# FP4 network between two attentions: where its inputs are quantized, and where the next attention's operands begin

## Chip, core and metric

The kernel runs on one core of a Trainium2 chip. The metric is the device time of one execution in microseconds. PE is the matmul engine (PEld its weight loads), DVE the vector engine, ACT the engine of activation functions, POOL the general-purpose engine, SP the engine from whose queue most DMAs are issued.

## The reference, cut to what matters

Eight batches of 512 tokens with 128 features go through four blocks; after each, the block's input is added and the sum is normalized.

```python
x = _layernorm(x + _L0_attn_ref(x, ...))   # 16 heads of 8, score bias by distance
x = _layernorm(x + _L0_ffn_ref(x, ...))    # FP4 network
x = _layernorm(x + _L1_attn_ref(x, ...))   # 16 heads of 8, no score bias
x = _layernorm(x + _L1_ffn_ref(x, ...))    # two layers of local attention and GEGLU

def fp4_quant_dequant(x):                  # blocks of 16 along the last dim
    scale = max(max(abs(xb)) / 6, 1e-12)
    xn = xb / scale
    return GRID[searchsorted(MID, abs(xn))] * sign(xn) * scale   # 0 .5 1 1.5 2 3 4 6
def _L0_ffn_ref(x, w_gate, w_up, w_down):  # 128 -> 352 -> 128
    q = fp4_quant_dequant
    h = silu(q(x) @ q(w_gate).T) * (q(x) @ q(w_up).T)
    return q(h) @ q(w_down).T
```

## The kernel before, in words

The activations stay on chip: `xn` and `xs` hold all eight batches, `xn` the normalized values and `xs` the sums before normalizing. The four blocks follow one another: `attention(0)`, `ffn0`, `attention(1)`, `ffn1`. A block opens its own pools of tiles on chip and closes them at its end, so the tiles of one block lie where those of the block before lay.

**Order.** Each engine has a queue. The program's scheduler chooses the order in a queue. An instruction wrapped in `keep_in_program_order` stays behind everything written before it for its engine; the attention's matmuls and transposes (`mm`, `tr`, lines 126 and 127) are wrapped so, as are the late loads on SP (`held`, line 78). The rest is free.

**An attention** (lines 121 to 352). For a batch, `begin_x` transposes `xn` to `xT`; `begin_qk` projects q and k, splits each into two parts on POOL (lines 167 and 168) and writes them to DRAM (`far`); `load_qk` reads them back into `qs_` and `ks_` in another layout; `begin_v` projects v into `va`, whose rest is zeros and a column of ones. Then a list of steps runs: eight per unit, four units per batch, 256 for eight batches, and 36 more in which the last units end. In step `s` the scores of one block of queries are made twice: PE makes `s_ps` and DVE takes its row maximum (line 239); 16 steps later PE makes the transposed scores `t_ps` and ACT takes the exponential into a tile `e` (line 245). `todo` holds what else a step does: the row of maxima is sent into `qs_` by a DMA from POOL's queue (line 257), the values are summed, the sums divided, projected, added and normalized (`end_o`, `end_y`). The next batch's operands begin ten steps ahead. The first batch's are made before the first step. Four PSUM banks of `p_t` are shared by `t_ps` and all the smaller products.

**The FP4 network** (lines 355 to 454). It loads the weights, quantizes them and transposes them into `wgu` and `wd`. `quantized` (line 361) does a blockwise quantization: DVE takes the maximum of each block (371) and makes scales and their inverses (372, 373, 375), POOL multiplies by the inverse (376), DVE isolates the exponent by an integer operation (377), makes from it a number to add and take away again (378, 379, 380), which rounds, and POOL multiplies by the scale (381). For each batch `begin` quantizes `xn`; `gated` transposes the result and makes the gate and up products, their product `h` and its quantization in two halves; `down` transposes it, multiplies by `wd`, adds and normalizes (by ACT, line 112). The next batch's `begin` and the down product of the batch before follow each `gated`.

Of the kernel before, what the change touches and what calls it, by code (L numbers as in the profile page):

```python
# [18 lines left out]
P = 128  # L19
B, S, D = 8, 512, 128  # L20
NT = S // P
G = 4
# [18 lines left out]
def body(ctx, tc, x, consts, rows, wa0, wa1, acols, bo, wf, wqkv, wo, w1, w2, cols, b2r, qs, ks, out):  # L41
# [77 lines left out]


    def attention(li, alibi, qs_, ks_, late=None):
# [6 lines left out]
        with ExitStack() as st:  # L128
# [11 lines left out]
            qb = const.tile([P, 1], F32, name="qb")  # L140
            nc.vector.tensor_tensor(qb, col[:, 0:1], col[:, 1:2], ALU.mult)
            va = []
            for i in range(2):
                v = const.tile([P, NT, 16, 32], F32, name=f"va{i}")
                nc.gpsimd.memset(v, 0.0)
                nc.gpsimd.memset(v[:, :, :, 8:9], 1.0)
                va.append(v)


            def begin_x(b, h):  # L150
                ps = bank("xt_ps")
                for c in range(NT):
                    tr(ps[:, c * P : (c + 1) * P], xn[:, b * NT + c, :], ident)
                h["xT"] = work.tile([P, S], F32, tag="xT", name="xT", bufs=1)
                nc.vector.tensor_copy(h["xT"], ps)

            def begin_qk(b, h, n):
                ps = bank("qk_ps")
                mm(ps, lhsT=w[:, n * P : (n + 1) * P], rhs=h["xT"], start=True, stop=True)
                t = work.tile([P, S], F32, tag=f"x{n}", name="x", bufs=1)  # L160
                if n == 0:
                    nc.scalar.activation(t, ps, AF.Identity, bias=qb, scale=col[:, 0:1])  # L162
                else:
                    nc.scalar.activation(t, ps, AF.Identity, bias=col[:, 2:3])
                parts = work.tile([P, 2, S], F32R, tag=f"hl{n}", name="parts", bufs=1)
                hi, lo = parts[:, 0, :], parts[:, 1, :]
                nc.gpsimd.tensor_copy(hi, t)  # L167
                nc.gpsimd.tensor_tensor(lo, t, hi.bitcast(F32), ALU.subtract)

                far = dram.tile([2, 2, 64, S], F32R, tag=f"far{n}", name="far")  # L170
                for j in range(2):
                    nc.sync.dma_start(
                        out=far[j].bitcast(F32).rearrange("a c t -> c a t"), in_=parts[64 * j : 64 * j + 64].bitcast(F32)
                    )
                h["far", n] = far

            def load_qk(b, h, n, part):

                dst, pp = (qs_, ks_)[n][b % 2], slice(4 * part, 4 * part + 4)
                for j in range(2):  # L180
                    both = h["far", n][j].bitcast(F32).rearrange("a (p d) t -> a d p t", d=8)
                    for r in range(4):
                        at = 64 * j + 8 * r
                        nc.sync.dma_start(
                            out=dst[at : at + 8, pp].bitcast(F32), in_=both[r // 2 if n == 0 else r % 2][:, pp]
                        )

            def begin_v(b, h):
                h["o"] = work.tile([P, NT, P], F32, tag="o", name="o", bufs=3)
                ps = bank("v_ps").rearrange("p (c d) -> p c d", c=NT)  # L190
                for c in range(NT):
                    mm(ps[:, c, :], lhsT=h["xT"][:, c * P : (c + 1) * P], rhs=w[:, W_V : W_V + P], start=True, stop=True)
                nc.scalar.copy(va[b % 2][:, :, :, 0:8], ps.rearrange("p c (h d) -> p c h d", d=8))
# [115 lines left out]
            batch, units = [{} for _ in range(B)], []  # L309
            for n in range(B * G):  # L310
# [7 lines left out]
                if g == 0 and b + 1 < B:  # L318

                    early = max(s - 10, 1)  # L320
                    later(early, begin_x, b + 1, batch[b + 1])
                    later(early + 2, begin_qk, b + 1, batch[b + 1], 0)
                    later(early + 4, begin_qk, b + 1, batch[b + 1], 1)
                    for part in range(2):
                        for j in range(2):
                            later(s + 6 + 12 * part + 2 * j, load_qk, b + 1, batch[b + 1], j, part)
                    later(s + 20, begin_v, b + 1, batch[b + 1])
                    later(s + 20, with_bias, b + 1)
                if g == G - 1:
                    later(z + 15, end_o, batch[b])  # L330
                    later(z + 18, end_y, b, batch[b])

            begin_x(0, batch[0])
            begin_qk(0, batch[0], 0)
            begin_qk(0, batch[0], 1)
            for part in range(2):
                for j in range(2):
                    load_qk(0, batch[0], j, part)
            begin_v(0, batch[0])
# [3 lines left out]
            with_bias(0)  # L343
            if late:
                late()
            for s in range(B * G * NU + LAG + 20):
# [3 lines left out]
                for f, a in todo.pop(s, []):  # L350
                    f(*a)
            assert not todo


    def ffn0():
        with ExitStack() as st:
            pool = lambda name, bufs, **k: st.enter_context(tc.tile_pool(name=f"f{name}", bufs=bufs, **k))
            const, work = pool("c", 1), pool("w", 2)
            p_g, p_t = pool("g", 2, space=PSUM), pool("t", 4, space=PSUM)

            def quantized(src, n, tag):

                nb = n // 16
                blocks = lambda t: t.rearrange("p (n k) -> p n k", k=16)
                over = lambda t: t.unsqueeze(2).broadcast_to([P, nb, 16])
                tile_ = lambda name, w: work.tile([P, w], F32, tag=f"{name}{tag}", name=name)
                sc, inv, y, m = tile_("sc", nb), tile_("inv", nb), tile_("y", n), tile_("m", n)  # L370
                nc.vector.tensor_reduce(sc, blocks(src), AX.X, ALU.max, apply_absolute_value=True)
                nc.vector.tensor_scalar(sc, sc, float(np.float32(1.0) / np.float32(6.0)), 1e-12, ALU.mult, ALU.max)
                nc.vector.reciprocal(inv, sc)

                nc.vector.tensor_scalar_mul(inv, inv, 1.0 - 2.0**-23)
                nc.gpsimd.tensor_tensor(blocks(y), blocks(src), over(inv), ALU.mult)
                nc.vector.tensor_single_scalar(m.bitcast(I32), y.bitcast(I32), 0x7F800000, ALU.bitwise_and)
                nc.vector.tensor_scalar(m, m, 1.0, 1.5 * 2.0**22, ALU.max, ALU.mult)
                nc.vector.tensor_tensor(y, y, m, ALU.add)
                nc.vector.tensor_tensor(y, y, m, ALU.subtract)  # L380
                nc.gpsimd.tensor_tensor(blocks(y), blocks(y), over(sc), ALU.mult)
                return y


            wgu = const.tile([P, 2, NI], F32, name="wgu")
            wd = const.tile([P, 3, D], F32, name="wd")
            wraw = const.tile([P, F_ALL], F32, name="wraw")
            nc.sync.dma_start(out=wraw, in_=wf)
            for j in range(2):
                wq = quantized(wraw[:, j * 3 * P : (j + 1) * 3 * P], 3 * P, "w")  # L390
                ps = p_t.tile([P, 3 * P], F32, tag="tr", name="w_ps")
                for c in range(3):
                    nc.tensor.transpose(ps[:, c * P : (c + 1) * P], wq[:, c * P : (c + 1) * P], ident)
                nc.scalar.copy(wgu[:, j, :], ps[:, 0:NI])
            wq = quantized(wraw[:, 6 * P : F_ALL], NI, "w")
            ps = p_t.tile([P, 3, P], F32, tag="tr", name="wd_ps")
            for c, (at, n) in enumerate(I_CH):
                nc.tensor.transpose(ps[0:n, c, :], wq[:, at : at + n], ident)
            for c, (at, n) in enumerate(I_CH):
                nc.scalar.copy(wd[0:n, c, :], ps[0:n, c, :])  # L400

            def begin(b):
                return quantized(xn[:, b * NT : (b + 1) * NT, :].rearrange("p c d -> p (c d)"), S, "x")

            def gated(b, xq):
# [6 lines left out]
                for half in range(2):  # L412
# [12 lines left out]
                    hq.append(quantized(h.rearrange("p t i -> p (t i)"), 2 * NI, "h"))  # L425
# [19 lines left out]
            xq = begin(0)  # L445
            before = None
            for b in range(B):
                hq = gated(b, xq)
                if b + 1 < B:
                    xq = begin(b + 1)  # L450
                if before:
                    down(*before)
                before = (b, hq)
            down(*before)
# [334 lines left out]
    with tc.tile_pool(name="ops", bufs=1) as ops:  # L789
# [14 lines left out]
        def first_late():  # L804
            constant_rows(1, held)
            load_late()

        constant_rows(0, nc.sync.dma_start)
        attention(0, True, qs_, ks_, first_late)
# [3 lines left out]
        ffn0()  # L813
        attention(1, False, qs_, ks_)
# [98 lines left out]
```

## Time and profile before

| | |
|---|---|
| Time of three runs, median (lowest to highest) | 2124.07 us (2123.54 to 2126.24) |
| The profiled execution's own time, its span | 2124.89 us, 2123.1 us |
| Mean granted TensorE clock | 0.914 of full speed |
| Busy, share of the span: PE, DVE, ACT, POOL | 82%, 71%, 54%, 39% |
| First attention, first to last step | about 36 to 562 us |
| FP4 network, with its weights | about 573 to 762 us |
| Second attention | about 762 to 1240 us |
| Last block | about 1240 to 2123 us |

Durations below come from the profiled execution. A row of a group names line, engine, operation, output and inputs by the program's names, the shapes and the count; then the busy time and the mean of one; then the idle time of its engine just before it and what ended that. A row of the timeline gives start and duration; an arrow in brackets names what the engine waited for. Instructions on one engine can overlap a little, so durations sum to more than busy time.

### The profile page before, as it was taken

What the parts mean: (1) busy time and instruction counts of PE and PEld (TensorE: products, weight loads), DVE (VectorE), ACT (ScalarE), POOL (GpSimd) and SP (SyncE); (2) the same over time, 40 slices, a digit from 0 to 9 for tenths busy, and PEclk for the clock granted to TensorE, in tenths of its full rate; (3) what the DMA queues carried; (4) which work ended last, traced back from release to release, by engine and by line L of the source; (5) the groups of instructions that cost most, each with busy time, mean ns of one, the idle gap of its engine ahead of it and who ended that gap; (6) DMA issues with size and microseconds to landing.
All of it is one profiled execution on the core that took longest, in us unless ns stands there. A gap on an engine that the chain in (4) does not pass through costs nothing.

```text
span 2123.1 us, 38263 instructions
## 1 busy us (share of the span) xinstructions
PE 1742.1 (82%) x14229; PEld 970.8 (46%) x14245; DVE 1501.2 (71%) x3156; ACT 1151.4 (54%) x2717; POOL 829.1 (39%) x880
## 2 busy tenths in 40 slices
PE   1899999999666549999999966888889889898894
PEld 0444444444244424333333333555655566565562
DVE  2577777777488737888888726777777777788752
ACT  0266666666422215777777723556656656656560
POOL 3312222212444451222221134465555555666653
PEclk6599999999877758999999967999999999999997
DMA  6532232220000024232221001111111111111110
GB/s 116 164 61 51 52 61 53 44 48 2 12 1 1 0 61 97 59 58 60 58 59 36 2 25 25 28 31 28 29 34 28 29 29 33 34 40 34 31 31 20
DMA packets 91628, 88.45 MB, mean 42 GB/s; under 512 B 45825, under 2 KB 57473, under 8 KB 91442
## 3 DMA queue, kind: packets, MB, share of 16 engines
q1 hardware_dynamic: 86752, 85.00, 18.2%
q8 instruction: 113, 1.85, 0.4%
q0 software_dynamic: 4096, 0.54, 0.2%
q14 instruction: 73, 0.60, 0.1%
q10 hardware_dynamic: 594, 0.47, 0.1%
HBM read 41.33 MB, written 18.87 MB: 28 GB/s over the span
## 4 chain that ended last, share of the span: by engine, by line
PE 23%; DVE 22%; ACT 13%; POOL 2%; issue 2%; DMA 1%; SPq 0%; ACTq 0%; POOLq 0%; DVEq 0%
ACT pw L463 8%; PE s_ps L126 7%; PE av L126 6%; DVE t L564 4%; DVE r L560 4%; DVE ss L568 3%; DVE m L624 3%; DVE m L239 3%; PE qk_ps L461 2%; ACT sq L463 2%; PE t_ps L126 2%; DVE nrm L587 1%; DVE u L739 1%; PE qk_ps L126 1%; PE p_ps L462 1%
## 5 line engine op out<-in xcount | busy, mean ns | idle before, releaser
L239 DVE TENSOR_REDUCE m<-s_ps 128x1 f32<-128x512 f32 x1024 | 647.8, 685 | 226.4 <-PE s_ps L126 117.6
L245 ACT ACTIVATE e<-t_ps 128x512 f32<-128x512 f32 x1024 | 552.8, 595 | 241.1 <-PE t_ps L126 235.8
L126 PE MATMUL s_ps<-k,q 63*128 63x512 f32 x1024 | 384.9, 511 | 106.9 <-DVE m L239 65.6
L126 PEld LDWEIGHTS s_ps<-k,q 63*128 63x128 f32 x1024 | 151.5, 192 | 399.7 <-DVE m L239 288.5
L463 ACT ACTIVATE pw<-sp,m,nrm 128x128 f32<-128x128 f32 x512 | 226.3, 462 | 180.2 <-DVE m L626 174.7
L126 PE MATMUL t_ps<-q,k 64*128 64x512 f32 x1024 | 286.4, 426 | 0.4 <-ACT e L245 0.2
L126 PE MATMUL av<-e,va 128*32 128x512 f32 x2048 | 275.2, 608 | 0.0
L257 POOL DMA_DIRECT2D q<-mt x128 | 68.4, 538 | 505.8 <-ACT mt L253 505.8
L637 POOL TENSOR_TENSOR pw<-pw,den 128x1024 f32<-128x1024 f32 x64 | 121.2, 1894 | 211.5 <-DVE den L636 164.6
L571 POOL TENSOR_TENSOR r<-r,t 128x1024 f32<-128x1024 f32 x64 | 150.9, 2358 | 98.8 <-DVE t L564 96.5
L560 DVE TENSOR_TENSOR r<-qk_ps,tab 128x512 f32<-128x512 f32 x128 | 87.4, 682 | 102.0 <-ACT sq L463 102.0
L461 PE MATMUL qk_ps<-wqkv_s,hT 128*128 128x512 f32 x256 | 140.2, 676 | 16.3 <-DVE t L564 15.5
L126 PEld LDWEIGHTS t_ps<-q,k 64*128 64x128 f32 x1024 | 127.1, 188 | 16.7 <-ACT e L245 16.5
L462 PE MATMUL p_ps<-cst,pw 128*128 128x128 f32 x512 | 76.4, 284 | 51.2 <-DVE xs L702 28.5
L463 ACT ACTIVATION_READ_ACCUMULATOR pw<-sp,m,nrm 128x1 f32 x512 | 106.9, 209 | 0.0
L464 ACT COPY v<-v_ps 128x512 f32<-128x512 f32 x64 | 37.5, 586 | 108.4 <-PE v_ps L461 108.4
L564 DVE TENSOR_TENSOR t<-qk_ps,tab 128x256 f32<-128x256 f32 x256 | 95.4, 414 | 0.0
L668 DVE COPY pT<-p_ps 128x512 f32<-128x512 f32 x128 | 84.3, 686 | 15.3 <-PE p_ps L462 14.7
L126 PEld LDWEIGHTS <-sel 64*128 64x128 bf16 x2048 | 69.3, 97 | 52.1 <-issue 39.3
L126 PE MATMUL s_ps<-tri,sel 64*128 64x64 bf16 x1024 | 91.7, 199 | 0.0
L167 POOL CAST parts<-x 128x512 fp32r<-128x512 f32 x32 | 19.4, 607 | 182.2 <-ACT x L162 176.8
L463 ACT ACTIVATE sq<-qk_ps 128x1024 f32<-128x1024 f32 x64 | 68.4, 1069 | 34.7 <-PE qk_ps L461 34.6
(161 smaller groups left out, 3229.1 us busy)
## 6 DMA issues: line engine op xcount, KB each, us to landing
far<-parts SPq DMA_DIRECT2D x64, 256.0 KB
q<-far SPq DMA_DIRECT2D x256, 64.0 KB
k<-far SPq DMA_DIRECT2D x256, 64.0 KB
ve<-v SPq DMA_DIRECT2D x112, 128.0 KB
xn<-in_x SPq DMA_DIRECT2D x8, 256.0 KB
q<-mt POOLq DMA_DIRECT2D x128, 4.0 KB, 2.8
hn<-xs SPq DMA_DIRECT2D x16, 128.0 KB
out<-xn SPq DMA_DIRECT2D x8, 256.0 KB
```

Source lines behind the costliest of these rows:

```text
L126: mm = lambda *a, **k: tc.keep_in_program_order(nc.tensor.matmul(*a, **k))
L239: nc.vector.tensor_reduce(u["m"][:, j, pp, blk : blk + 1], ps[j], AX.X, ALU.max)
L245: nc.scalar.activation(e, ts[j], AF.Exp, scale=float(SLOPES[2 * vp + j]) if alibi else 1.0)
L257: nc.gpsimd.dma_start(out=q[at : at + 1, 2 * g : 2 * g + 2, :].bitcast(F32).rearrange("o a (c t) -> o (a c) t", t=P), in_=mt[8 * j : 8 * j ...
L461: mm = lambda *a, **k: tc.keep_in_program_order(nc.tensor.matmul(*a, **k))
L462: tr = lambda *a, **k: tc.keep_in_program_order(nc.tensor.transpose(*a, **k))
L463: act = lambda *a, **k: tc.keep_in_program_order(nc.scalar.activation(*a, **k))
L560: nc.vector.tensor_tensor(heads(r[:, n]), heads(ps[:, n]), cos.unsqueeze(1).broadcast_to([P, HEADS, DH]), ALU.mult)
L564: nc.vector.tensor_tensor(heads(t2[:, n])[:, :, a : a + 32], heads(ps[:, n])[:, :, 32 - a : 64 - a], sin[:, a : a + 32].unsqueeze(1).broad ...
L571: nc.gpsimd.tensor_tensor(r, r, t2, ALU.add)
L637: nc.gpsimd.tensor_tensor(pw.rearrange("p s r k -> p (s r) k"), pw.rearrange("p s r k -> p (s r) k"), den.rearrange("p s r -> p (s r)").un ...
L668: nc.vector.tensor_copy(h["pT"][:, s], ps)
```

## The change

`quantized` moves out of the network, gets its buffers from its caller, and writes its result where the caller says. The integer operation is replaced by an absolute value on ACT, and the two constants after it change:

```diff
-                nc.vector.tensor_single_scalar(m.bitcast(I32), y.bitcast(I32), 0x7F800000, ALU.bitwise_and)
-                nc.vector.tensor_scalar(m, m, 1.0, 1.5 * 2.0**22, ALU.max, ALU.mult)
+        nc.scalar.activation(m, y, AF.Abs)
+        nc.vector.tensor_scalar(m, m, 1.5, 2.0**22, ALU.max, ALU.mult)
```

The weights are quantized in the first attention, before its first step, in nine of the 13 `e` tiles; their transposes use banks of `p_t` and are not wrapped. The network's own copies of this are gone.

```diff
+    def tokens(b):
+        return xs[:, b * NT : (b + 1) * NT, :].rearrange("p c d -> p (c d)")
+    def quantize_tokens(b, y, m, small):
+        quantized(xn[:, b * NT : (b + 1) * NT, :].rearrange("p c d -> p (c d)"), S, y, m, tokens(b), small)
+    def quantize_weights(piece, small, bank):
+        for j in range(3):
+            n = 3 * P if j < 2 else NI
+            raw, y, m = piece(), piece(), piece()
+            nc.sync.dma_start(out=raw[:, 0:n], in_=wf[:, 3 * P * j : 3 * P * j + n])
+            quantized(raw[:, 0:n], n, y[:, 0:n], m[:, 0:n], y[:, 0:n], small)
+            ps = bank("w_ps")
...
+        def first_late(piece, small, bank):
             constant_rows(1, held)
+            quantize_weights(piece, small, bank)
             load_late()
```

The first attention takes a `tail`: from step 256 on, every third step, one batch's `xn` is quantized into `xs`, seven batches in all, with the two `parts` buffers of the q and k projections in turn as work space. The eighth is done at the network's start. `gated` reads `tokens(b)`.

```diff
+                if tail and s >= B * G * NU and (s - B * G * NU) % 3 == 0:
+                    t = (s - B * G * NU) // 3
+                    tail(t, work.tile([P, 2, S], F32R, tag=f"hl{t % 2}", name="parts", bufs=1).bitcast(F32), work)
...
+        def first_tail(t, ym, small):
+            if t < B - 1:
+                quantize_tokens(t, ym[:, 0, :], ym[:, 1, :], small)
```

`begin_x`, `begin_qk`, `load_qk` and `begin_v` move, with the same body but for the tile `o`, into `operand_steps`, which both an attention and the network call. The network begins the second attention's first two batches with unwrapped matmuls:

```diff
+                if b in (3, 5):
+                    n, h = len(batch), {}
+                    batch.append(h)
+                    begin_x(n, h)
+                    begin_qk(n, h, 0)
+                    begin_qk(n, h, 1)
+                    for part in range(2):
+                        for j in range(2):
+                            load_qk(n, h, j, part)
+                    begin_v(n, h)
```

The second attention then begins only the batches from the third on (`begun <= b + 1 < B`) and adds the bias for both begun batches ahead of its steps. The tiles `va`, `wgu`, `wd` and `qb` move to the pool of `qs_` and `ks_`, which is opened once for both attentions and the network; `va` is cleared once, written after the clearing of `qs_` and `ks_`, instead of once in each attention.

## The prediction

> **What bounds the kernel now.** I read the 40 slices of the page first: PE falls from 9 tenths to 5 and 4 around slices 11 to 14 and its granted clock falls with it, so the FP4 network and its two borders are the thin place. Then the busy times in stretches cut at the borders, whose columns are length, PE, PEld, DVE, ACT, POOL busy (instructions), clock, DMA share, GB/s:
>
> ```profile
> 36.00:543.00 507.00, 449.82 (x4285) 222.29 (x4285) 363.86 (x647) 294.82 (x565) 108.18 (x162) 0.94 0.28 60
> 543.00:562.00 19.00, 18.17 (x164) 6.83 (x163) 1.10 (x4) 15.81 (x34) 3.51 (x3) 1.00 0.01 1
> 573.00:594.00 21.00, 3.66 (x15) 2.85 (x16) 19.69 (x46) 1.52 (x6) 9.88 (x12) 0.50 0.00 0
> 594.00:757.00 163.00, 104.15 (x444) 74.94 (x442) 128.87 (x278) 45.92 (x117) 74.44 (x72) 0.76 0.00 1
> 757.00:783.00 26.00, 7.02 (x20) 4.41 (x19) 3.33 (x9) 3.70 (x7) 20.53 (x40) 0.57 0.28 83
> 783.00:806.00 23.00, 20.15 (x38) 8.27 (x37) 16.93 (x28) 3.00 (x4) 6.82 (x11) 0.50 0.42 113
> ```
>
> The reader sees four limits. The first attention's loop has PE busy 89% of 507 us. Its last steps leave DVE almost free (1.10 of 19 us). From 573 to 594 DVE alone works, on the weights and the first batches. The network has DVE busy 79% of 163 us, PE 64% at a clock of 0.76. From 757 to 783 PE stands. The timeline shows what opens each stage:
>
> ```profile
> 573.38 1.01 DVE L371 TENSOR_REDUCE sc<-wraw 128x24 f32<-128x384 f32 x2 [4.79 <-POOL xn L116]
> 594.62 1.19 PE L419 MATMUL gp<-wgu,xqT 128*128 128x352 f32 x2
> 762.07 1.90 DVE L137 COPY bvb<-acol 128x128 f32<-128x128 f32 x1 [3.87 <-ACT xn L112]
> 782.73 0.76 PE L126 MATMUL s_ps<-k,q 63*128 63x512 f32 x1 [12.94 <-DMA q<-far]
> ```
>
> Each stage's pools open only when the stage before has read its last tile (the first reduce of the network waits for POOL's `xn`, `bvb` for ACT's `xn`). After that come 21.2 us to the first gate matmul and 20.7 us to the first score, the latter behind projections and the trip of q and k through DRAM. Inside the network, the groups by shape (busy, mean ns):
>
> ```profile
> L379 DVE TENSOR_TENSOR y<-y,m 128x704 f32<-128x704 f32 x16 | 18.4, 1152 | 0.0
> L377 DVE TENSOR_SCALAR m<-y 128x704 int32<-128x704 int32 x16 | 13.3, 829 | 9.0 <-POOL y L376 9.0
> L379 DVE TENSOR_TENSOR y<-y,m 128x512 f32<-128x512 f32 x8 | 7.3, 915 | 0.2
> ```
>
> **The order is not the text's order.** This line is the residual plus bias of all eight batches (32 = 8 x 4), done at the second attention's start, though seven of them are written 20 steps into each batch:
>
> ```profile
> 771.71 13.18 POOL L197 TENSOR_TENSOR xs<-xn,crow 128x128 f32<-128x128 f32 x32
> ```
>
> So whatever isn't tied by `keep_in_program_order` goes out as soon as its inputs and its buffer are there. I use this for every moved part.
>
> **The Trainium skill.** *SBUF — State Buffer*, section "SBUF: two separate sides": VectorE instructions in a two-port mode or with two SBUF inputs exclude GpSimd's from a shared port pair, for a whole instruction. The trace agrees: L379 has a median of 0.87 us over its forms and took 1.87 us at 684.81, beside a POOL multiply at 684.39 that ran 1.53 us. *ScalarE: Activation LUTs*, section "Table sets: the hidden batching unit": abs is in every set as filler. No `Abs` is in this trace; it agrees so far that Copy and Identity run among the network's Silu with one table load. *TensorE: Matmul & The Clock Gate*, Part 1: an idle PE is held at half clock. Agrees: 0.50 at 783 to 806, where a score matmul took 0.76 us against a mean of 0.51.
>
> **The change, part by part.** Against the profiled execution's own time, 2124.89 us (span 2123.1 and 1.8 around it), which is 0.8 above the median of the runs.
>
> *Start.* The two `va` tiles are now cleared in the pool of q and k, whose clears waited for a cast that ended at 8.7 us; before, POOL did `va` at 0.72, in idle time. Now POOL does k (to 15.7), then `va` (2 x 1.82 + 2 x 0.20 = 4.0), then the q and k parts, which open SP's trip to DRAM at 19.87 and the first score at 35.76. **+4.** Bounds: 0 if the parts go first; +9 if the 560 KB of weights also hold up the first loads (4.9 us at the 115 GB/s of the first 36 us).
>
> *Weights.* Three DMAs on SP, free of order, so ahead of the constants (SP idles from 1.6 to 12.3). Their DVE rows sum to 10.7 us, less 2.5 for the integer row, 8.2; POOL 5.4; PE 9 transposes, 2.7; ACT three Abs and five copies, 3.0. DVE is busy 9.2 of the first 36 us, so all hides there: **0**. Without that cover see rival C: the step loop's first matmul is tied behind the last weight transpose. What it removes is counted at the border.
>
> *Seven batches.* A 512-wide quantization takes on DVE 0.67 + 0.18 + 0.35 + 0.17 + 0.42 + 0.69 + 0.69 = 3.2 us uncontended (without L377), on POOL 2.2, on ACT one Abs of about 0.6 (Copy 128x512: 0.585). Written for steps 256 to 274, they need only `xn` of their batch and a `parts` buffer, whose last user sits at 422.5; I expect most of them between 420 and 543, in the loop, not in the idle tail. There 22 us of DVE meet 14 of 60 us idle while PE is busy 92% (55.2 of 60 at 370 to 430). An oT copy of 0.68 at 407.96 pushed the next reduce not at all. **+3**; bounds 0 (all in gaps) and +15 (two thirds of 22).
>
> *Border to the network.* Its pools still wait for `xn` at 573.3. Then only xqT (transposes 1.1, copy 0.58) stands before the first gate matmul: 575.0 for 594.62, **-19.6**; bounds -21 and -10 (a late seventh quantization).
>
> *Network.* DVE rows from 573 to 762 sum to 171 us, their union is 150 (instructions overlap by 12%). Seven of eight 512-wide quantizations go: 7/8 of 39.8 = 34.8. L377 of the 704-wide goes: 13.3. Together 48 x 0.88 = 42, of which 10 lay before 594 (19.7 less the weights' 9.4). So 129 - 32 = 97, and two xT copies: 98.5. Added: Abs 128x704 on ACT, 16 x 0.745 (452 ns for 352 and 585 for 512 give 0.83 ns per element) = 12, so ACT has about 62; the two begun batches, PE 8, POOL 7.5, ACT 4, all beside DVE; 8 far and 64 loading DMAs on SP, idle here, DMA share 0.00. If DVE's idle falls from 34 to 31 (ACT's seven waits for xq, 23.9 us in all, fall away; a third engine joins each quantization's chain), 98.5 + 31 = 130 for 163: **-33**. Bounds: -49 (idle 15: fill and drain alone) and -10.
>
> *Border to the second attention.* `bvb` still waits for ACT's `xn`; then bvb, its matmul and the first score, 763 for 782.7: -19.7. Reducing ran without gap from 797 at 0.61 us each, so 16 steps take 32 x 0.61 = 20 for the 26.1 from 782.73 to 808.82: -6. Batch 1's v matmuls go from the loop: -1.2. PE stays at half clock there. Two batches' bias sums (8 x 0.45 on POOL) are wanted only at a batch's end: 0. **-27**; bounds -20 and -29.
>
> Sum: 4 + 3 - 19.6 - 33 - 27 = -72.6. Own time 2052.3, median **2051**.
>
> **Rivals.**
> A (0.70): as summed; its own range is 2024 to 2075.
> B (0.12): the network is bound by the chain POOL, ACT, DVE, POOL, not by DVE's load. For: it waits 38.7 us on `y L376 <- DVE inv`. Against: gate matmuls of the next batch no longer wait. Network -10: 2074.
> C (0.08): the weights come behind SP's second constant rows, landing near 52 us; then 8 us of quantizing hold back the tied matmuls, first score near 62 for 35.8. For: those DMAs stand first in the text. Against: nothing ties them. +26 in place of +4: 2073.
> D (0.04), slower: the moved quantizations stall the loop through the in-order queues. POOL waits up to 14.1 us in front of its mask-row DMA (L257) for ACT's mt; a multiply queued behind it holds Abs, that holds DVE's next step, and the reduces behind it. At a full unit of eight steps each, 7 x 14.1 = 99 for the 3: 2147. It decides from 75.6 / 7 = 10.8 us per quantization. Against: POOL is busy 12 of 60 us there.
> E (0.06): Abs isn't in the sets, so each reloads a table twice (1.28 us): 16 x 2.57 = 41 us on ACT in the network, 2092 if none hides. That the begun operands are not used at all would be worth +27, 2078, and belongs here.
>
> **The numbers.** The range holds A, B, C and half of E: 2022 to 2086. Only D is slower, by more than 0.2% (4.2 us), about what a measurement of this kernel can tell from no change: 0.95, 0.01, 0.04.
>
> **What would show it.** Right: first score near 40 us; L371 on `xn` between 420 and 545; the first gate matmul within 3 us of POOL's last `xn`; no L377; network near 130 us with DVE over 70%; no wait for `q<-far` at the second attention's start. Wrong: table loads above 40 in number, POOL multiplies behind L257 with DVE idle over 2 us, a network over 150 us.

## The result and the profile after

The changed kernel takes 2111.57 us (median of 12 runs, 2108.58 to 2122.29), the kernel before 2124.53 us (12 runs). The ratio is 0.9943, with a 95% interval of 0.9931 to 0.9955: faster by 13 us where 73 were forecast. The profiled execution took 2111.14 us, its span is 2109.1 us.

Busy times in stretches cut at the new borders. The columns are length, then PE, PEld, DVE, ACT, POOL busy (instructions), clock, DMA share, GB/s:

```profile
36.00:71.30 35.30, 1.66 (x6) 0.98 (x6) 6.13 (x14) 1.47 (x3) 11.20 (x23) 0.50 0.87 221
71.30:593.00 521.70, 465.93 (x4289) 228.93 (x4288) 383.50 (x696) 300.21 (x575) 117.12 (x159) 0.92 0.23 45
593.00:612.00 19.00, 17.97 (x163) 6.74 (x162) 1.10 (x4) 15.85 (x33) 3.73 (x3) 1.00 0.01 1
624.70:768.10 143.40, 101.89 (x472) 74.68 (x472) 97.64 (x228) 60.81 (x139) 72.42 (x70) 0.87 0.15 34
768.10:774.20 6.10, 0.70 (x5) 0.51 (x4) 1.35 (x6) 1.65 (x4) 1.70 (x4) 0.50 0.00 1
774.20:794.20 20.00, 19.62 (x37) 9.05 (x36) 19.06 (x33) 1.54 (x2) 14.32 (x34) 0.50 0.44 83
```

The first stretch is new: PE does almost nothing until 71.3, where before its first score came at 35.76. In the last steps (third stretch) DVE is as idle as before, 1.10 of 19 us: none of the moved quantizations lies there. The network's DVE load fell from 128.9 to 97.6 us, yet it still takes 143.4 us. The two borders have shrunk to 0.7 and 6.1 us. The timeline of PE shows the openings (start, duration, engine, line, operation, and in brackets the idle time before it and what ended it):

```profile
61.83 0.90 PE L158 MATMUL w_ps<-cst,e 128*128 128x128 f32 x3 [31.58 <-POOL e L139]
70.55 0.90 PE L162 MATMUL w_ps<-cst,e 128*128 128x128 f32 x3 [7.82 <-POOL e L139]
71.38 0.79 PE L222 MATMUL s_ps<-k,q 63*128 63x512 f32 x2
...
624.68 1.54 PE L436 MATMUL gp<-wgu,xqT 128*128 128x352 f32 x2 [4.54 <-ACT xqT L427]
...
774.19 1.22 PE L222 MATMUL s_ps<-k,q 63*128 63x512 f32 x3
```

PE waits 31.6 us for the first quantized weights, with the first score queued behind the last of their transposes. The gate products follow the last `xn` (624.00) by 0.7 us, the second attention's first score the network's last product by 6.1.

DVE's groups in the network's stretch (mean ns, then the idle time before, and what ended it):

```profile
L137 DVE TENSOR_TENSOR y<-y,m 128x704 f32<-128x704 f32 x16 | 17.7, 1108 | 0.1
L441 DVE TENSOR_TENSOR h<-up,si 128x352 f32<-128x352 f32 x32 | 16.2, 514 | 27.8 <-ACT si L440 14.2 <-PE up L436 11.7 <-POOL y L134 1.9
L136 DVE TENSOR_SCALAR m<-m 128x704 f32<-128x704 f32 x16 | 9.4, 585 | 6.3 <-ACT m L135 6.1
```

The integer row is gone, the sums cost as before, and 27.8 us of DVE's 45.8 idle ones stand in front of `h`.

Stage by stage, from the two timelines:

| us | before | after | moved by | forecast |
|---|---|---|---|---|
| first attention, end of its last `xn` | 573.34 | 624.00 | +50.7 | +7 |
| to the first gate product | 21.28 | 0.68 | -20.6 | -19.6 |
| network, to its last `yp` | 162.4 | 143.4 | -19.0 | -33 |
| to the first score | 25.7 | 6.1 | -19.6 | -19.7 |
| first score to first `t_ps` | 26.1 | 20.0 | -6.1 | -6 |
| the rest | 1314.3 | 1314.9 | +0.7 | -1.2 |

So two steps failed: the first attention by 44 us, the network by 14. ACT's copies of `mt`, one per unit, date the first: they run 18.4 us late at the first unit and 17.3 from the third on, then jump by 6.3 (near 190), 3.6 (near 260), 6.2, 8.3 and 1.9 (471 to 546) and 6.3 (581 to 592), to 49.9.

### The profile page after: what moved, and what is told of

It reads as the page before. It is cut to its first block, busy times and chain, and to the rows that moved or that the text cites. A ratio compares the mean times of both kernels' runs of the same rounds, so it can differ in the third digit from the quotient of the medians.

```text
span 2109.1 us, 38268 instructions
## 1 busy us (share of the span) xinstructions
PE 1744.7 (83%) x14229; PEld 972.7 (46%) x14245; DVE 1477.4 (70%) x3128; ACT 1169.4 (55%) x2744; POOL 827.9 (39%) x876
## 4 chain that ended last, share of the span: by engine, by line
PE 24%; DVE 24%; ACT 14%; POOL 4%; issue 3%; DMA 1%; SPq 0%; ACTq 0%; POOLq 0%; DVEq 0%
ACT pw L492 8%; PE s_ps L222 7%; PE av L222 6%; DVE t L593 4%; DVE r L589 4%; DVE ss L597 3%; DVE m L653 3%; DVE m L287 3%; ACT sq L492 2%; PE qk_ps L490 2%; PE t_ps L222 2%; DVE u L768 1%; DVE nrm L616 1%; PE o_ps L223 1%; ACT L492 1%
## 5 line engine op out<-in xcount | busy, mean ns | idle before, releaser
L222 PE MATMUL s_ps<-k,q 63*128 63x512 f32 x1024 | 391.9, 516 | 82.7 <-DVE m L287 80.2
L222 PE MATMUL t_ps<-q,k 64*128 64x512 f32 x1024 | 292.3, 432 | 0.3 <-ACT e L293 0.2
L222 PE MATMUL av<-e,va 128*32 128x512 f32 x2048 | 281.6, 621 | 0.0
L490 PE MATMUL qk_ps<-wqkv_s,hT 128*128 128x512 f32 x256 | 140.3, 676 | 16.3 <-DVE t L593 15.5
L491 PEld LDWEIGHTS p_ps<-cst,pw 128*128 128x128 f32 x512 | 56.6, 144 | 67.4 <-DVE xs L731 25.2
```

Source lines behind the costliest of these rows:

```text
L222: mm = lambda *a, **k: tc.keep_in_program_order(nc.tensor.matmul(*a, **k))
L490: mm = lambda *a, **k: tc.keep_in_program_order(nc.tensor.matmul(*a, **k))
L491: tr = lambda *a, **k: tc.keep_in_program_order(nc.tensor.transpose(*a, **k))
```

## The experiments

Theory for the start: the second and third weight piece waited for their tiles, not for the bus. Theory for the jumps: quantizations put into the loop make DVE's queue stand. The rival for the start was the clearing of `va`; for the loop, that the work itself doesn't fit, or that the weights' delay is all. SP's queue in the changed kernel, first all three loads of the weights (lowest, median and highest duration in ns, then the first and the last start), then the rows around the late ones:

```profile
L153 SPq DMA_DIRECT2D e<-in_wf x3: 512/1891/2642, 1.7 to 51.7; - x3
...
46.49 2.58 SPq L78 DMA_DIRECT2D q<-rowq  x1
49.11 0.60 SPq L78 DMA_DIRECT2D k<-rowk  x1
49.76 4.58 SPq L153 DMA_DIRECT2D e<-in_wf  x2
54.38 4.78 SPq L78 DMA_DIRECT2D xn<-in_x  x7
```

One of three pieces goes out at once, at 1.7 us; two go out behind the second constant rows. And this is the first of the jumps, on DVE and then on all engines in stretches:

```profile
189.34 0.68 DVE L287 TENSOR_REDUCE m<-s_ps 128x1 f32<-128x512 f32 x1
192.58 0.69 DVE L129 TENSOR_REDUCE sc<-xn 128x32 f32<-128x512 f32 x1 [2.55 <-POOL xn L116]
193.18 1.28 DVE L287 TENSOR_REDUCE m<-s_ps 128x1 f32<-128x512 f32 x2
```

```profile
192.00:196.00 4.00, 1.45 (x13) 0.70 (x13) 3.39 (x10) 1.09 (x2) 2.38 (x3) 0.87 0.06 15
196.00:205.00 9.00, 8.83 (x53) 3.81 (x55) 4.49 (x8) 3.26 (x6) 0.00 (x0) 0.50 0.41 92
```

A block maximum needs only `xn` and a small buffer, so it went into the queue right at the end of the first batch (step 58 of 292), and DVE stood 2.55 us until POOL had made `xn`. The row maxima behind it came late, PE was busy 1.45 of 4 us, and then its clock was 0.50 for 9 us. The block maxima at 260.22 and 581.46 waited 2.56 and 3.62 us in the same way. The other four quantizations look different. In the largest jump (8.3 us) DVE waited no more than 1.2 us at a time; steps of two quantizations stood in front of its row maxima, and PE waited 6.35 us for one of these:

```profile
517.09 1.28 DVE L287 TENSOR_REDUCE m<-s_ps 128x1 f32<-128x512 f32 x2
...
521.13 1.43 DVE L137 TENSOR_TENSOR parts<-parts 128x512 f32<-128x512 f32 x1
...
524.37 1.43 DVE L138 TENSOR_TENSOR parts<-parts 128x512 f32<-128x512 f32 x1
525.72 1.28 DVE L287 TENSOR_REDUCE m<-s_ps 128x1 f32<-128x512 f32 x2
...
526.46 0.79 PE L222 MATMUL s_ps<-k,q 63*128 63x512 f32 x1 [6.35 <-DVE m L287]
```

**e1_loads_first**

```diff
+        raws = []
+        for j in range(3):
+            raws.append(piece())
+            nc.scalar.dma_start(out=raws[j][:, 0:n], in_=wf[...])
         for j in range(3):
-            raw, y, m = piece(), piece(), piece()
-            nc.sync.dma_start(out=raw[:, 0:n], in_=wf[...])
+            raw, y, m = raws[j], piece(), piece()
```

> The three raw weight pieces get their e tiles and their DMAs (on ACT's queue) before any of the other six tiles is handed out; everything else is as after the change. Theory (the second and third piece waited for tiles that are handed out in order, so they went out at 49.8 us, behind SP's second constant rows, and the tied first score waited for the last weight transpose): first score between 36 and 45 us for 71.4, the first attention ends 13 to 18 us earlier, 2095 us or so. Rival (the start is late because the clearing of va on POOL, and the projections behind it, hold up the first score): first score stays above 55 us, 2105 or more.

2095.02 us, ratio 0.9857 (0.9835 to 0.9878). First score at 37.91, the first attention ends at 608.52, 15.5 us earlier. Its timeline, the loads on ACT's queue, then PE:

```profile
2.60 2.33 ACTq L154 DMA_DIRECT2D e<-in_wf  x3
...
36.11 0.90 PE L166 MATMUL w_ps<-cst,e 128*128 128x128 f32 x3 [3.02 <-POOL e L139]
37.91 0.76 PE L226 MATMUL s_ps<-k,q 63*128 63x512 f32 x1 [0.91 <-DMA k<-far]
```

The score now waits for `far`, no longer for the weights; the later jumps stay (4.2, 3.6, 6.1, 8.3, 2.0, 6.3). The clearing of `va` is as in the changed kernel, so it did not hold the first score back to 71.4. The explanation is that tiles under one tag are handed out in the order of the text, so that the second piece's tile came after the first's `y` and `m`; e9 shows such an order in the network. The edit changes the order of the tiles and the queue at once, and the two were not tried apart; for the tiles speaks that the first piece left SP's queue at 1.7 us.

**e2_tied_tail**, for the moved quantizations:

```diff
-        nc.vector.tensor_reduce(sc, blocks(src), ...)
+        tie(nc.vector.tensor_reduce(sc, blocks(src), ...))
...
-                quantize_tokens(t, ym[:, 0, :], ym[:, 1, :], small)
+                quantize_tokens(t, ym[:, 0, :], ym[:, 1, :], small, tc.keep_in_program_order)
```

> The block maximum that opens each of the seven moved quantizations is kept behind what was written before it for DVE, so none can begin before its step. Theory (the quantizations, hoisted into the loop by a free order, stalled DVE's queue there; some 30 us of the first attention): no block maximum of xn before the last 36 steps, the shifts at 192, 260 and 471 to 545 us gone, the last xn of the first attention at 594 to 600 for 624.0, 2081 to 2088 us. Rival (the last steps have no room either: the seven chains over POOL, ACT, DVE and POOL take some 3.5 us each one after the other and end after the loop): network starts late instead, 2100 or more.

2099.25 us, 0.9879 (0.9865 to 0.9894). The delay is 17.8 from the third unit to the last: all six jumps are gone. The last 36 steps, though, now take 43 us for 29.5, so that the attention ends at 604.80. Theory right on the loop; the rival holds for 13 us of the 32.

**e3_no_tail**

```diff
-        attention(0, True, qs_, ks_, va, [], first_late, first_tail)
+        attention(0, True, qs_, ks_, va, [], first_late)
...
+            def begin(b):
+                y, m = temps(S)
+                quantize_tokens(b, y, m, work)
...
                 hq = gated(b)
+                if b + 1 < B:
+                    begin(b + 1)
```

> The seven quantizations go back into the network, one batch ahead as before the change; the moved weights, the begun operands and ACT's absolute value stay. Theory (they cost 32 us in the loop and save less than that in the network): the first attention ends near 592 for 624.0, first gate matmul some 8 to 10 us behind it (one whole quantization), network 155 to 165 for 143 us, so 2095 to 2110. Rival (the loop is late because of the weights alone): the first attention still ends past 610 and the time is above 2115.

2153.20 us, 1.0136 (1.0119 to 1.0153). The first attention ends at 594.22 as expected, its delay constant at 20.9. The network is a miss: 204.9 us. PE's longest waits there, from the first gate product on (total, times, longest):

```profile
PE xq_ps L425 <- POOL xs L139: 65.6, 5, 16.9
```

Each batch's tokens come late. e8 and e9 take this up.

**e4_both**: e1 and e2 together.

> The edits of e1_loads_first and e2_tied_tail together. If the two causes are separate they add: first attention ends near 580 (573.3 before the change, 624.0 after it), 2064 to 2072 us. If both edits mend the same delay (the shift of the start and that of the loop absorb each other), 2080 or more.

2079.62 us, 0.9785 (0.977 to 0.98). The gains add, and a little more (15.5 and 19.2 alone, 36.9 together): the attention ends at 587.09, with a delay of 0.2 to 0.4 us from the third unit to the last, and another 13.4 in the last steps. It missed the forecast (580) by those. With the weights early the start is thus 0.4 us late here and 4.0 in e1, all causes together, so `va`'s clearing can't cost more than that; it was not taken out alone. e4_both is the base of most of what follows.

**e5_buffers** and **e6_integer**, both in the network alone:

```diff
-        ... for t, n_ in (("sc", 2), ("inv", 1)))
+        ... for t, n_ in (("sc", 4), ("inv", 4)))
```

```diff
-        nc.scalar.activation(m, y, AF.Abs)
-        nc.vector.tensor_scalar(m, m, 1.5, 2.0**22, ALU.max, ALU.mult)
+        nc.vector.tensor_single_scalar(m.bitcast(I32), y.bitcast(I32), 0x7F800000, ALU.bitwise_and)
+        nc.vector.tensor_scalar(m, m, 1.0, 1.5 * 2.0**22, ALU.max, ALU.mult)
```

> e4_both, and the network's quantizations get four buffers each for the scales and their inverses instead of two and one. Theory X (the network is slower than forecast, 144 for 130 us, because a quantization's maximum waits until the one two before it has been multiplied out, so chains of POOL, ACT and DVE hardly overlap): network 128 to 136 us, total 2064 to 2072. Theory Y (it is ACT's in-order queue, in which silu, absolute values and copies wait for one another): network 141 to 145, total 2077 to 2082.

> e4_both, and in the network the exponent of h is isolated on DVE by the integer operation again (16 x 0.83 us more on DVE, 16 absolute values of 0.79 us less on ACT); the moved quantizations keep ACT's. Theory Y (ACT's queue): DVE's load rises from 98 to about 111 us and the network still shortens, 132 to 140 us, total 2068 to 2075. Theory X (buffers): 143 to 150 us, total 2079 to 2085.

e5: 2080.90 us, 0.9787 (0.9766 to 0.9807), network 145.4 for 144.4. e6: 2089.29 us, 0.9824 (0.9805 to 0.9843), network 155.2 with 105.3 us of DVE for 97.9. Both theories fall: X by e5, Y by e6. `Abs` on ACT earns about 10 us (9.7 of the total, 10.8 of the network), of the 13 that were forecast for its DVE row.

**e7_clears**, in the network's loop instead of ahead of it:

```diff
+                if b < 4:
+                    tc.keep_in_program_order(
+                        nc.gpsimd.memset(ks_[b // 2][64 * (b % 2) + 32 : 64 * (b % 2) + 48].bitcast(F32), 0.0)
+                    )
```

> e4_both, and the four clears of 16 rows of the k tiles on POOL (3.5 us each, two of them between the last quantizations, each beside a DVE instruction of 3.1 us) are issued in the network after its first four batches. Theory (in the last 36 steps, 42.8 for 29.4 us, POOL's queue is what the quantizations and the last normalization wait in): the last xn of the first attention at 578 to 582 for 587.1, network at most 3 us longer, total 2071 to 2076. Rival (DVE's order there, the last division behind the next quantization's steps, is what counts): at most 3 us earlier, and the clears cost the network as much, 2078 to 2084.

2079.02 us, 0.9785 (0.9767 to 0.9803): the attention ends 3.9 us earlier, the network takes 5.2 more. What it moved is seen in e4_both, DVE first, then POOL:

```profile
565.50 3.19 DVE L136 TENSOR_SCALAR parts<-parts 128x512 f32<-128x512 f32 x1 [1.84 <-ACT parts L135]
...
573.96 3.08 DVE L136 TENSOR_SCALAR parts<-parts 128x512 f32<-128x512 f32 x1
...
564.90 3.50 POOL L862 MEMSET k<- 16x4096 f32 x1
573.25 3.51 POOL L862 MEMSET k<- 16x4096 f32 x1
```

A 0.43 us instruction of DVE took 3.1 to 3.2 beside each clear; in e7, with no clear there, all seven took 0.43 or less. Neither expectation holds in both its figures, and nothing is gained by moving the clears.

**e8_no_tail_buffers** is e3 with e5's buffers. **e9_no_tail_tags** is e3 with another tag for token quantizations (`own` is "x" for them and empty for the rest):

```diff
-        ... small.tile([P, 2 * NI // 16], F32, tag=t, name=t, bufs=n_)
+        ... small.tile([P, 2 * NI // 16], F32, tag=t + own, name=t, bufs=n_)
```

> e3_no_tail (all eight token quantizations in the network, 204.9 us there), with the four and four buffers of e5_buffers. Theory X: the token quantization of the next batch is handed its scale buffers behind both of h's, so gated waits for it (PE waited 65.6 us on it); with the buffers the network takes 150 to 165 us, total 2098 to 2115. Theory Y (ACT's queue does it): 195 us or more, total above 2140.

> e3_no_tail (all eight token quantizations in the network, 204.9 us there), with the buffers for the scales of a token quantization under a tag of their own, two and one as those of h. The number of buffers being no cause (four instead of two: 208.3 us), theory Z: tiles of one tag are handed out in the order of the text, so a batch's token quantization can't begin before the h of the batch before it exists; with a tag of its own it runs ahead. Network 150 to 165 us, total 2097 to 2115. Rival (the 35 us of token work on DVE and POOL itself): above 190 us, total above 2138.

e8: 2157.36 us, 1.0154 (1.0136 to 1.0173), network 208.3. e9: 2106.68 us, 0.9918 (0.9904 to 0.9933), network 160.2, and from the first gate product on PE no longer waits for `xs`. Not the number of buffers but the shared name cost 45 us: the next batch's tokens could not take a buffer before both halves of the present `h` had. In e9 the quantizations stay in the network and it is some 5 us faster than the change, late weights and all (the two intervals just touch).

**e10_late_norm**

```diff
-                layernorm(work, b, on_act=True)     # in down
...
                 if before:
                     down(*before)
                 before = (b, hq)
+                if b > 1:
+                    layernorm(work, b - 2, on_act=True, tie=tc.keep_in_program_order)
```

The last two batches' normalizations follow the loop.

> e4_both, and in the network a batch's normalization is written one batch later, its instructions on ACT kept behind what was written before. Theory (ACT's queue stands up to 5.4 us at a time in front of xn for POOL's four small instructions, 17.7 us in all, with silu, absolute values and copies of the next batch behind it, which DVE and PE then wait for): the wait of xn on mr falls below 5 us, network 130 to 138 us for 144.4, two normalizations at its end add 2 us to the border, total 2068 to 2074. Rival (the chain of each batch is what counts, ACT's wait lies beside it): network 142 to 147 us, total 2079 to 2084.

2074.43 us, 0.9767 (0.9752 to 0.9781), network 139.7. ACT's wait of `xn` on `mr` fell from 17.7 to 3.0 us, but the network gained 4.7: most of that wait seems to have lain beside other work. Neither expectation's network figure holds.

**e11_split**: e1, and each quantization in three tied parts.

```diff
+                t, r = divmod(s - 66, 32)
+                if tail and 0 <= t < B - 1:
+                    if r == 0:
+                        ym = work.tile(...)
+                        part = tail(t, ym, work)
+                    if r in (0, 2, 3):
+                        next(part)
```

> The weights' loads first as in e1_loads_first; each moved quantization is cut in three parts, written at steps 2, 4 and 5 of a unit some 8 steps after its xn is made (block maximum to the first multiply; absolute value; the rest), each part kept behind what was written before it. Theory (a quantization in the loop costs where DVE, POOL or ACT stand in front of one of its instructions whose input isn't there; with its input there each lies in the gaps): 6 x 0 to 1.5 us in the loop, the last 36 steps back at 30 to 33 us from 42.8, first attention ends at 574 to 583, total 2066 to 2075. Rival (22 us of DVE work and POOL's use of DVE's port cost in the loop whatever the order): loop longer by 15 us or more, 2081 or above.

2072.37 us, 0.9757 (0.9742 to 0.9771). The last steps, cut at the last `mt`, in e11_split and then in e4_both:

```profile
555.30:584.70 29.40, 20.81 (x182) 9.06 (x174) 5.99 (x19) 16.13 (x32) 14.67 (x12) 0.96 0.00 1
```

```profile
544.30:587.10 42.80, 25.90 (x182) 11.62 (x174) 32.24 (x61) 19.74 (x38) 26.22 (x24) 0.80 0.00 1
```

The tail is back at 29.4 us. The last `mt` is 11.4 us late, of which 0.9 stand from the start; the loop is 10.5 longer, some 1.8 for each of six quantizations, a little above what was expected and far below the 4.7 that each of seven cost in the change (32.6). Their place in the order, not DVE's work as such, was most of it; what the 1.8 consist of stays open.

**e12_none_begun**

```diff
-                if b in (3, 5):
+                if b in ():
```

> e4_both, but no batch of the second attention is begun in the network; the attention makes all its operands itself. Theory (the forecast's border, and that the begun operands lie beside other work): from the network's last product to the first score 25 us for 6.1, the first 16 steps 6 us longer, network shorter by 0 to 4 us; total 2101 to 2106 for 2079.6. Rival (the begun operands hold the network up by as much as they save): total 2080 to 2090.

2087.35 us, 0.9821 (0.9804 to 0.9837). The border is 23.2 us for 6.1, near the 25 expected. But the network takes 129.4 us, so the rival's total holds: of what the begun operands save behind the network only 7.7 us remain. e12_none_begun and then e4_both,

```profile
593.50:722.90 129.40, 97.35 (x440) 72.20 (x440) 93.25 (x226) 56.97 (x133) 63.39 (x62) 0.84 0.00 1
```

```profile
588.80:733.20 144.40, 100.98 (x472) 73.27 (x472) 97.93 (x228) 60.39 (x139) 72.66 (x70) 0.88 0.16 33
```

The begun operands add 4.7 us of DVE, 9.3 of POOL, 3.6 of PE and 3.4 of ACT, and 15.0 to the length. DVE's waits in front of `h` go from 7.5 us without them (6.7 for `si`, 0.2 for `up`, 0.6 for POOL) to 24.9 with them (14.2, 10.1, 0.6), the largest again first without, then with them:

```profile
DVE h L445 <- ACT si L444: 6.7, 5, 2.6
```

```profile
DVE h L445 <- ACT si L444: 14.2, 5, 8.0
DVE h L445 <- PE up L440: 10.1, 5, 6.8
```

Not all of these 17.4 us lengthen the network: in front of the sums `xs` DVE waits 9.0 us less (10.8 for 19.8), and its idle time as a whole rises by 10.3, from 36.2 to 46.5. The first begun batch in e4_both, POOL, then ACT, then DVE:

```profile
651.26 1.38 POOL L139 TENSOR_TENSOR y<-y,sc 128x704 f32<-128x704 f32 x1
652.73 0.23 POOL L104 TENSOR_SCALAR rstd<-stats 128x4 f32<-128x4 f32 x1
652.91 0.61 POOL L191 CAST parts<-x 128x512 fp32r<-128x512 f32 x1
653.49 1.04 POOL L105 TENSOR_TENSOR rstd<-rstd,half 128x4 f32<-128x4 f32 x1
654.50 1.26 POOL L192 TENSOR_TENSOR parts<-x,parts 128x512 fp32r<-128x512 f32 x1
655.72 0.20 POOL L108 TENSOR_TENSOR mr<-stats,rstd 128x4 f32<-128x4 f32 x1
...
656.28 1.65 ACT L112 ACTIVATE xn<-xs,mr,rstd 128x128 f32<-128x128 f32 x4 [5.38 <-POOL mr L109]
657.84 0.79 ACT L444 ACTIVATE si<-gp 128x352 f32<-128x352 f32 x2
...
658.31 0.95 DVE L445 TENSOR_TENSOR h<-up,si 128x352 f32<-128x352 f32 x2 [7.97 <-ACT si L444]
```

The splits of q and k lie between the four small instructions of a normalization. ACT stands in front of `xn` for them, `si` stands behind `xn`, DVE waits 7.97 us for `si`.

**e13_parts_tied**, for the network's begun batches:

```diff
-            nc.gpsimd.tensor_copy(hi, t)
+            tc.keep_in_program_order(nc.gpsimd.tensor_copy(hi, t))
```

**e14_begun_last** and **e16_one_begun** change the line of e12 to `if b in (6, 7):` and `if b in (3,):`.

> e4_both, and in the network POOL's first copy of each split of a begun q or k is kept behind what was written before it, so behind the normalization of the batch before. Theory P (at the first begun batch 5 us of these splits lay between the four small instructions of a normalization; ACT stood 5.4 us in front of xn, DVE then 8.0 us in front of h): the wait of xn on mr falls by 4 us or more, network 137 to 140 us for 144.4, total 2072 to 2077. Rival Q (the begun steps cost in PE's and ACT's order and in the PSUM banks): network 143 to 147 us, total 2078 to 2083.

> e4_both, with the two batches begun after the seventh and the eighth batch's gate products instead of the fourth's and the sixth's. Theory Q: only down products and normalizations stand behind the second, one batch's gate products behind the first, so of the 15 us that begun steps cost the network some 5 to 9 remain: network 135 to 139 us for 144.4, first score still 6 to 8 us after its last product, total 2070 to 2076. Theory P: the splits still lie ahead of two normalizations, network 141 to 145 us, total 2077 to 2082.

> e4_both, with one batch begun in the network, after the fourth. If the cost is one batch's steps each: network 136 to 138 us for 144.4 (two) and 129.4 (none); the border stays at 6 us since the first score needs batch 0 alone; its second batch is begun by the attention, 3 to 6 us in the first steps; total 2074 to 2079 for 2079.6. If the first begun batch alone costs (its splits ahead of a normalization): network 143 to 145 us and 2080 to 2086.

e13: 2076.75 us, 0.9770 (0.9753 to 0.9788), network 141.7. e14: 2074.03 us, 0.9756 (0.9738 to 0.9773), network 139.6. e16: 2077.39 us, 0.9774 (0.9756 to 0.9792), network 137.8. So one begun batch costs 8.4 us and the second 6.6, and a place with less behind it gives 4.8 back. For the splits' place e13 gives 2.7, which is not clear of noise: the same network took 143.4, 145.7, 146.7 and 144.4 us in the change, e1, e2 and e4, and the intervals of e13 and e4 overlap. In e13 the splits did go behind the normalization at the first begun batch (ACT's wait 3.45 us for 5.38), yet all waits of `xn` on `mr` together were 19.7 us for 17.7, so theory P isn't borne out. e16's border stays at 6.1. The begun steps' cost is shown; how it divides between the splits, PE's order, ACT's order and the shared PSUM banks stays open.

**e15_split_late** joins e10 and e11; **e17_joined** adds e14.

> The edits of e10_late_norm and e11_split together (early loads, quantizations in three tied parts in the loop, normalization one batch later in the network). If both gains add (5.2 and 7.2 us of 2079.6): 2066 to 2069 us. If the network's gain depended on how it starts: 2071 to 2074.

> e15_split_late with the two batches begun after the seventh and eighth batch's gate products as in e14_begun_last. If the gains add (e14's 5.6 us to e15's 2067.7): 2061 to 2064 us, network 132 to 135 for 138.2. If both remove the same wait (ACT in front of a normalization with a begun batch's splits ahead of it on POOL): 2066 to 2069.

e15: 2067.67 us, 0.9726 (0.9705 to 0.9746), network 138.2. e17: 2063.06 us, 0.9719 (0.9706 to 0.9732), 48.5 us faster than the change. In both the gains added as expected. The network of e17, with both batches begun in it (the profiled execution was the fastest of five, 2057.35 us):

```profile
584.10:715.10 131.00, 98.17 (x472) 70.04 (x472) 104.65 (x229) 61.32 (x139) 72.91 (x70) 0.88 0.11 29
```

DVE carries 104.7 us in it, more than in the change (97.6), and it is 12.4 us shorter.

## Why the prediction was wrong

**Start and weights, forecast +4 and 0, measured +17.3 together.** The failed step is "free of order, so ahead of the constants". One of the three loads did go ahead; two went out at 49.76 us, by the account above because their tiles were not free of order, and the tied first score stood behind them. Rival C had the mechanism (weights behind the second constant rows, tied matmuls behind the weights); its reason against, "nothing ties them", was the same mistake. It put the first score near 62 (71.38 measured) and the price at 26. Of the 35.6 us at the first score, 18.4 were left at the first unit, since the kernel before waited there too, for `xn` from DRAM (PE's wait before the change; total, times, longest):

```profile
PE xt_ps L127 <- DMA xn<-in_x: 15.9, 1, 15.9
```

With early weights all that is left at the start is 0.4 to 4.0 us, within the bounds set for `va`'s clearing.

**Seven batches, +3 forecast, +32.6 measured.** Place and order were foreseen for most ("between 420 and 543, in the loop"), the price was not. The step that failed is the price "+3" with its bound "+15 (two thirds of 22)": it set DVE's work against DVE's idle time and put nothing for what the work makes wait behind it. The six jumps sum to 32.6 us, more than the 22 us of work. At three places DVE stood in front of a block maximum whose `xn` wasn't there: 2.55 us of waiting at 192.58 went with 6.3 of delay, part of it at half clock. At the four between 471 and 546 the quantizations' own steps stood in front of the row maxima, so there DVE's load counts too, by where it was put. The maxima at 192 and 260 came so early since they need no `parts` buffer. The precedent I used, one copy that pushed nothing, had its input there. Rival D named the in-order queue and was set aside; its place (POOL's mask-row DMA) and price (14.1 us each) were not those found. e11 shows that with tied parts whose inputs are there the loop pays 1.8 each. The Trainium skill, *TensorE: Matmul & The Clock Gate*, section "Architectural detail: the array is 16× 32×32, not 1× 128×128", says that ACT and DVE are "strict FIFO"; the row at 192.58 agrees. I had used the free order of the program's scheduler, and not what follows where a queue is then strict.

**Border to the network, -19.6: right, -20.6.** The seventh quantization was in time.

**Network, -33 forecast, -19.0 measured.** DVE's load was right: 98.5 forecast, 97.6 measured. The idle term failed, 31 forecast, 45.8 measured, through "beside DVE": the begun operands, priced at nothing, cost 15.0 us (e12), and without them the network takes 129.4 for the 130 forecast. That match is partly luck: there DVE is busy 93.3 us and idle 36.2, for 98.5 and 31. Rival B (the chain, not the load) gave some 153; it was nearer on the length (143.4) but for another reason, as e12 has the same chains and takes 129.4, and e6, with one engine less in the chain of `h` and more load on DVE, takes 155.2.

**Border to the second attention, -19.7 and -6: right, -19.6 and -6.1.** What it saves is paid for in part in the network, see above. No wait for `q<-far` is left. No table was loaded for `Abs` (32 loads in all, as before), so rival E's first half is out, and the operands were used.

Sum: 50.7 - 20.6 - 19.0 - 19.6 - 6.1 + 0.7 = -13.9, against a difference of the spans of 14.0. Of the 58.6 us missing, 13.3 are the start, 29.6 the loop and 14.0 the network; the remaining 1.7 are small differences in the other terms.

## What to carry to other kernels

An instruction moved into an in-order queue can cost more than its duration, by what it makes that queue wait for and by what then comes late behind it: give it a place where its inputs are there already, and tie it there. Look at names as at data: tiles of one tag, handed out in the order of the text, bind what is otherwise free (a shared tag cost 45 us in e3; tiles handed out early, with the loads in another queue, gained 15.5 at the start). "Lies beside the busiest engine" is no price until it is seen what the moved work stands in front of on each of its other engines.

## What the hardware showed that I had not expected

A gap of a few microseconds cost PE more than itself: busy 1.45 of 4 us near 192, it then ran at 0.50 for 9 us, where its matmuls took 0.79 us for 0.49. The Trainium skill, *TensorE: Matmul & The Clock Gate*, section "What's actually happening", lowers the clock after an idle window; here PE was not wholly idle. Nor was it idle where the clock stayed low: at the second attention's start it was busy 19.62 of 20 us at 0.50, and 20.15 of 23 us before the change, where the prediction read the 0.50 as that of an idle PE. What else holds the clock down no run here shows. And a one-input operation of DVE (128x512, 0.43 us alone) took 3.19 us beside a POOL clear of 3.50 and ended 0.3 us after it: that fits the shared port pair of the Trainium skill, *SBUF — State Buffer*, section "SBUF: two separate sides", which the one of the two that starts first holds for its whole instruction, seen here with a clear that reads nothing. Of DVE's one-input instructions that section names those in a two-port mode; whether this one was in such a mode, the trace doesn't say.
